# Two gated convolution layers and a linear attention: the normalization between layers, split into three chunks and one

## The chip, the cores and the metric

The kernel runs on one core of one Trainium2 chip, in float32. The metric is the device time of one execution in microseconds (us), as the median of several executions.

## The reference

The input has 512 channels of 64 x 64 pixels. Four layers follow each other, each as `x = x + layer(_gn(x))`, where `_gn` normalizes groups of 16 channels over all pixels:

```python
def _gn(v, G=32, eps=1e-5):
    g = v.reshape(B_, G, C_ // G, H_, W_)
    m = jnp.mean(g, axis=(2, 3, 4), keepdims=True)
    s = jnp.var(g, axis=(2, 3, 4), keepdims=True)
    return ((g - m) / jnp.sqrt(s + eps)).reshape(v.shape)

# layer 0: attention with 8 heads over 4096 pixels
# layers 1 and 2, gated convolutions:
fused = conv1x1(x, w_in, b_in)                  # 512 -> 1024 channels
pwa, abc = fused[:, :128], fused[:, 128:]
dw0, dw1, dw2 = dwconv7(abc, dw_w, dw_b)        # 7x7 per channel, 128 + 256 + 512 channels
h = pwa * dw0
h = conv1x1(h, pw0_w, pw0_b) * dw1
h = conv1x1(h, pw1_w, pw1_b) * dw2
return conv1x1(h, w_out, b_out)                 # 512 -> 512
# layer 3: linear attention; begins with qkv0 = conv1x1(x, w_qkv) * s_qkv + b_qkv (512 -> 768)
```

## The kernel before

The activations stay on the chip the whole time, as `X[128, 4, 4096]`: the 512 channels are four chunks of 128 partitions, the pixels are eight blocks of 512. A group of 16 channels lies inside one chunk, so the chunks can be normalized independently of each other.

**The normalization** is not written out as a pass of its own. The mean is taken off the pixels in place (`centered.take`, L355 on ACT, L357 on DVE and GpSimd), and the reciprocal deviation is multiplied into the weights of the layer that follows (L363 and L366 for `w_in`, L1316 for `w_qkv`). What both need comes from `_group_params`: the statistics of each chunk are aggregated on DVE (L95), a small product with a mask gives the negative mean of each group, `less` (L106, L108), another gives the variance (L115), then a square root on ACT (L121), a reciprocal and a correction step on DVE (L123 to L129) give `rstd`. The chain alternates between DVE, TensorE and ACT and is run once for each layer over all four chunks.

**The end of a gated layer.** The last of its output products take the hidden chunks `h5` and `h6` (`output` with chunks 5 and 6, after the gate products `g[5] + g[6]`). There is one output product for each of eight pixel blocks and four output chunks, 32 in all, blocks outside and chunks inside. After each, DVE adds the result to X (L1167) and takes the statistics of that block (L1169). A chunk's statistics are complete only with the last block.

**The beginning of the next layer.** `_group_params` runs; then the weights are scaled and the first four blocks of products are made, each over the four input chunks (`fused`, L842: `w_in[0]` and `w_in[1]`, or `w_qkv[0]` and `w_qkv[1]`, times pixel blocks 0 and 1). The other pixel blocks are centred meanwhile (`taken`). Products over the other blocks follow in a scheme with seven products instead of eight (`_Seven`), which needs sums of weights (L406) and differences of pixel blocks (L419) from DVE. The products become planes in DRAM, from which the depthwise convolution reads them back.

**The order of the work.** Each engine executes its own list in order. The lists come from a scheduler that reorders the program text by readiness; the big products of these layers are kept in the order of the text (`keep_in_program_order`), the small ones of the normalization are not. A product instruction of this kernel in float32 is executed as two TensorE instructions in the profile. DMAs are issued on three queues: SP (weights, taps, planes read back), ACT (planes written, `s_qkv`, `w_proj`) and GpSimd. Buffers come from pools that are stacked on each other; a new pool's buffers lie where closed pools' buffers were, and wait for those that used them last.

Of the whole kernel, the boundary between the two gated layers lies at about 2762 us of the profile, that between the second gated layer and the linear attention at about 3250 us.

Of the kernel before, what the change touches and what calls it, by code (L numbers as in the profile page):

```python
# [10 lines left out]
FP = mybir.dt.float32  # L11
AF = mybir.ActivationFunctionType
# [4 lines left out]
P = 128  # L17
# [75 lines left out]
def _aggregate(nc, mv, stats, c):  # L93

    nc.vector.bn_aggr(mv[:, c, :], stats[:, c, :, :].rearrange("p b s -> p (b s)"))  # L95


def _group_params(nc, small, psum, stats, gmask, known=None, mv=None):


    if mv is None:
        mv = small.tile([P, NC, 2], FP, tag="gn_mv", name="gn_mv")
        for c in range(NC):
            _aggregate(nc, mv, stats, c)
    ps = psum.tile([P, BLK], FP, tag="mm", name="gn_ps")
    nc.tensor.matmul(ps[:, 0:NC], gmask, mv[:, :, 0], start=True, stop=True)  # L106
    less = small.tile([P, NC], FP, tag="gn_less", name="gn_less")
    nc.vector.tensor_scalar(less, ps[:, 0:NC], -1.0, None, ALU.mult)  # L108

    d = small.tile([P, NC], FP, tag="gn_d", name="gn_d")  # L110
    nc.vector.tensor_add(d, mv[:, :, 0], less)
    nc.vector.tensor_mul(d, d, d)
    nc.vector.tensor_add(d, d, mv[:, :, 1])
    ps = psum.tile([P, BLK], FP, tag="mm", name="gn_ps")
    nc.tensor.matmul(ps[:, 0:NC], gmask, d, start=True, stop=True)  # L115
    if known is not None:
        known(less)
    a = small.tile([P, NC], FP, tag="gn_a", name="gn_a")
    nc.vector.tensor_scalar(a, ps[:, 0:NC], GN_EPS, None, ALU.add)
    s = small.tile([P, NC], FP, tag="gn_s", name="gn_s")  # L120
    nc.scalar.activation(s, a, AF.Sqrt)  # L121
    r = small.tile([P, NC], FP, tag="gn_r", name="gn_r")
    nc.vector.reciprocal(r, s)  # L123

    t = small.tile([P, NC], FP, tag="gn_t", name="gn_t")
    nc.vector.tensor_mul(t, r, r)
    nc.vector.tensor_mul(t, t, a)
    nc.vector.tensor_scalar(t, t, -0.5, 1.5, ALU.mult, ALU.add)
    nc.vector.tensor_mul(r, r, t)  # L129
    return less, r  # L130


@with_exitstack
def trunk_kernel(ctx: ExitStack, tc: tile.TileContext, a: dict, out: bass.AP):
# [56 lines left out]

    stats = _gated_convs(tc, a, X, vcol, vall, gmask, small, new_stats, centered, stats, mv, F)
    _linear_attention(tc, a, X, vcol, vall, ident, gmask, small, centered, stats, F3, Z, out)


# [132 lines left out]
class _Centered:  # L328
# [4 lines left out]
    def __init__(self, tc, small):  # L333
# [3 lines left out]
        self.nc.vector.memset(self.offset, 0.0)  # L337

    def first(self, view):


        def known(less):
            self.less = less
            for c in range(NC):
                self.take(view(c), c, (None, None, self.nc.gpsimd, self.nc.vector)[c])

        return known
# [10 lines left out]

    def scaled(self, w, rstd, eng):

        if eng is self.nc.scalar:
            for c in range(NC):
                eng.activation(w[:, c], w[:, c], AF.Copy, scale=rstd[:, c : c + 1])  # L363
        else:
            shape = [P, NC, w.shape[-1]]
            eng.tensor_tensor(w, w, rstd.unsqueeze(2).to_broadcast(shape), ALU.mult)  # L366
        return w


def _normalize(tc, X, gmask, small, psum, st):  # L370

    nc = tc.nc
    for b in range(NB):
        for c in range(NC):
            nc.vector.bn_stats(st[:, c, b, :], X[:, c, ts(b, BLK)])
    less, rstd = _group_params(nc, small, psum, st, gmask)
    for b in range(NB):
        for c in range(NC):
            xs = X[:, c, ts(b, BLK)]
            nc.vector.tensor_scalar(  # L380
                xs, xs, less[:, c : c + 1], rstd[:, c : c + 1], ALU.add, ALU.mult
            )
# [94 lines left out]
def _attention_pairs(tc, a, X, QO, gmask, small, centered, stats, mv, okay):  # L477
# [19 lines left out]
    with tc.tile_pool(name="att1", bufs=1) as p1, tc.tile_pool(  # L497
# [12 lines left out]
        for b in range(NB):  # L510
            for c in range(NC):
                nc.vector.bn_stats(stats[:, c, b, :], X[:, c, ts(b, BLK)])
        _, rstd = _group_params(
            nc, small, ps_mm, stats, gmask, centered.first(lambda c: X[:, c, 0:BLK])
        )


# [297 lines left out]
class _PlaneConv:  # L815
# [28 lines left out]
    def pixels(self, x, k):  # L844


        split = XW // self.f.phx
        v = x.rearrange("p (y h x n) -> p y h x n", y=XH, h=split, x=XW // split)
        py, px = divmod(k * self.pair, self.f.phx)
        return v[:, py, :, px : px + self.pair, :].rearrange("p h x n -> p h (x n)")  # L850

# [138 lines left out]


@with_exitstack
def _gated_convs(ctx, tc, a, X, vcol, vall, gmask, small, new_stats, centered, stats, mv, F):
# [11 lines left out]
    pc = _PlaneConv(ctx, tc, FORM, F, ps_cv, NL, 4, False)  # L1005

    for layer in ("L1", "L2"):
        pre = f"{layer}_conv_"

        def weights(name, i):  # L1010
# [9 lines left out]
        nc.sync.dma_start(out=pw1, in_=a[f"{layer}_pw1"])  # L1020
        _, rstd = _group_params(
            nc, small, ps_mm, stats, gmask, centered.first(lambda c: pc.pixels(X[:, c, :], 0)), mv
        )
        stats, mv = new_stats(), None

        centered.scaled(w_in[0], rstd, nc.vector)
        centered.began()
        for w in w_in[1:]:
            centered.scaled(w, rstd, nc.scalar)

# [7 lines left out]

        def taking(w, k):

            return product(lambda c: w[:, c, :], [pc.pixels(X[:, c, :], k) for c in range(NC)])

        def taken(k):
            for c in range(NC):
                centered.take(pc.pixels(X[:, c, :], k), c)

        def fused(i, k):

            put(i, k, taking(w_in[i], k), None)

# [165 lines left out]
        g = [blocks(gate, i) for i in range(NDW)]  # L1216
        fused(0, 0)
        taken(1)
        fused(1, 0)
        for b in (2, 3):  # L1220
            taken(b)
        fused(0, 1)
        for _ in made[0, 1]:
            pass
        fused(1, 1)
        for k in range(1, NB // 2):
# [8 lines left out]
        convolve(6, [], g[4] + outputs(4))  # L1235
        for _, f in g[5] + g[6] + outputs(5, 6):
            f()
    return stats


@with_exitstack
def _linear_attention(ctx, tc, a, X, vcol, vall, ident, gmask, small, centered, stats, F, Z, out):

# [10 lines left out]

    lq = ctx.enter_context(tc.tile_pool(name="lq", bufs=1))

    s_qkv = lq.tile([P, NQKV, P], FP, tag="s_qkv", name="s_qkv")
    nc.scalar.dma_start(
        out=s_qkv.rearrange("p i m -> p (i m)"),
        in_=bass.AP(a["L3_s"].tensor, a["L3_s"].offset, [[0, P], [1, NQKV * P]]),  # L1260
    )
    w_proj = lq.tile([P, NC, C], FP, tag="w_proj", name="w_proj")
    nc.scalar.dma_start(out=w_proj, in_=a["L3_w_proj"])
    ksum = small.tile([P, NC, NB], FP, tag="ksum", name="ksum")
# [33 lines left out]
    with ExitStack() as st:  # L1298
        wp = st.enter_context(tc.tile_pool(name="lw", bufs=1))
        w2p = st.enter_context(tc.tile_pool(name="lw2", bufs=4))  # L1300
        tmp = st.enter_context(tc.tile_pool(name="ltmp", bufs=5))
        kvp = st.enter_context(tc.tile_pool(name="kv", bufs=33))
        ps_vk = st.enter_context(tc.tile_pool(name="ps_vk", bufs=1, space=PSUM))
        ps_mm = st.enter_context(tc.tile_pool(name="ps_mm", bufs=4, space=PSUM))
        pc = _PlaneConv(st, tc, f, F, ps_mm, NL, 4, True)

        def weights(i):
# [5 lines left out]

        def scaled(i, w):
            for c in range(NC):
                nc.vector.scalar_tensor_tensor(  # L1316
                    w[:, c], w[:, c], rstd[:, c : c + 1], s_qkv[:, i], ALU.mult, ALU.mult
                )
            return w
# [15 lines left out]

        _, rstd = _group_params(
            nc, small, ps_mm, stats, gmask, centered.first(lambda c: pc.pixels(X[:, c, :], 0))
        )

        def product(w, hs):  # L1340
# [5 lines left out]
        for i, w in enumerate(w_qkv):  # L1346
            scaled(i, w)
        centered.began()

        def taken(k):  # L1350
            for c in range(NC):
                centered.take(pc.pixels(X[:, c, :], k), c)

        def put(i, k, ps, more=None):
# [5 lines left out]
            )  # L1360

        def fused(i, k):
            w = w_qkv[i]
            ps = product(lambda c: w[:, c, :], [pc.pixels(X[:, c, :], k) for c in range(NC)])
            put(i, k, ps)

# [71 lines left out]
        def more_weights():  # L1438
# [3 lines left out]
        dve, pool = nc.vector, nc.gpsimd  # L1442
        made = [
            lambda: fused(0, 0),
            lambda: [taken(1), summed(0), fused(1, 0)],
            lambda: [taken(2), taken(3), fused(0, 1)],
            lambda: [[p() for p in differences(1, dve)], fused(1, 1)],
        ]
        made += group(0, 1, centers(2) + differences(2, dve))
        made += group(0, 2, centers(3) + differences(3, dve))  # L1450
# [149 lines left out]

        fill(33)
        convs([(0, 0), (1, 0)], fills(5, 5, 5, 5))
# [225 lines left out]
```

## Time and profile before

| | us |
|---|---|
| median of 3 executions | 3862.63 |
| lowest and highest | 3862.24, 3863.66 |
| the profiled execution | 3863.14 |
| its span | 3861.4 |
| mean granted TensorE clock in it | 0.996 of full speed |

The profile is that of one execution. Its page gives the busy time of each engine and the costliest groups of instructions; further views are the waits (who waited for whom, in a stretch of time), the timeline (instructions in order of time, equal ones merged with their number behind an x), and a table of stretches with the busy time of each engine and the granted clock. PE is TensorE's matmuls, PEld its weight loads, DVE VectorE, ACT ScalarE, POOL GpSimd, SP the queue of SyncE. A line number is that of the code before. A wait for several events is put down to the one that came last.

### The profile page before, as it was taken

How to read it: one execution, taken by the hardware profiler on the slowest of the kernel's cores; microseconds unless marked ns; L12 is line 12 of the kernel's file. 1: busy time of each engine (PE TensorE's matmuls, PEld its weight loads, DVE VectorE, ACT ScalarE, POOL GpSimd, SP SyncE). 2: the span in 40 equal slices, each digit the busy share in tenths (PEclk: the TensorE clock that was granted, in tenths of full speed). 3: DMA queues.
4: the chain of work that ended last, by engine and by line, in shares of the span. 5: the costliest groups of instructions: out<-in, count | busy, mean ns of one | idle time of the engine just before them, and what ended most of it. 6: DMA issues, size and time to landing. Idle time of an engine off the chain costs nothing. (4 is left out here: it accounts for less than half of the span.)

```text
span 3861.4 us, 81785 instructions
## 1 busy us (share of the span) xinstructions
PE 3776.3 (98%) x35438; PEld 1674.7 (43%) x35438; DVE 2647.3 (69%) x3194; ACT 2063.5 (53%) x2987; POOL 112.2 (3%) x94
## 2 busy tenths in 40 slices
PE   6999999999999999999999999999999999999999
PEld 4533335333354333353333334554445544455544
DVE  5678774777766777747776757766677667575535
ACT  3677763777736777636665655663256632354210
POOL 0000000000000000000000000000000000122110
PEclk9999999999999999999999999999999999999999
DMA  2000000000000000000000015762056721463334
GB/s 99 9 1 1 1 1 9 1 1 1 1 1 9 1 1 1 1 9 1 1 1 1 1 49 167 201 199 75 17 161 191 202 73 42 151 181 96 94 96 141
DMA packets 194012, 221.56 MB, mean 57 GB/s; under 512 B 13400, under 2 KB 138584, under 8 KB 193520
## 3 DMA queue, kind: packets, MB, share of 16 engines
q1 hardware_dynamic: 166832, 157.12, 14.7%
q10 hardware_dynamic: 26784, 59.11, 4.2%
q8 instruction: 280, 4.59, 0.5%
q14 instruction: 84, 0.69, 0.1%
q0 software_dynamic: 32, 0.06, 0.0%
HBM read 156.46 MB, written 59.77 MB: 56 GB/s over the span
## 5 line engine op out<-in xcount | busy, mean ns | idle before, releaser
L664 ACT ACTIVATE pt<-ps_s,A 128x512 f32<-128x512 f32 x2048 | 1284.5, 686 | 536.6 <-PE ps_s L656 529.0
L741 DVE TENSOR_TENSOR acc<-acc,pt 128x1024 f32<-128x1024 f32 x960 | 1177.8, 1227 | 324.0 <-ACT pt L664 296.1
L676 PE MATMUL av<-pt,V 64*64 64x512 f32 x8192 | 1112.3, 590 | 0.9 <-ACT pt L664 0.9
L656 PE MATMUL ps_s<-O,K 64*64 64x512 f32 x8192 | 1111.4, 589 | 0.0
L676 PEld LDWEIGHTS av<-pt,V 64*64 64x64 f32 x8192 | 339.5, 133 | 557.6 <-issue 525.8
L656 PEld LDWEIGHTS ps_s<-O,K 64*64 64x64 f32 x8192 | 333.9, 133 | 554.5 <-issue 307.6
L920 ACT COPY S<-S 32x1295 f32<-32x1295 f32 (+1 forms) x272 | 341.4, 1256 | 218.2 <-DMA S<-F 107.4
L842 PEld LDWEIGHTS ps_cv<-S,T 64*32 64x32 f32 x13824 | 193.2, 105 | 109.6 <-issue 70.5
L842 PE MATMUL ps_cv<-S,T 64*32 64x128 f32 x13824 | 231.5, 272 | 4.4 <-DVE turned L974 1.5
L842 PE MATMUL ps<-diff,w_sum 128*128 128x512 f32 x492 | 231.1, 601 | 3.4 <-DVE w_sum L406 2.0
L842 PE MATMUL ps<-h,w_out_L 128*128 128x512 f32 x512 | 228.7, 599 | 1.5 <-DVE X L1163 1.4
L419 DVE TENSOR_TENSOR diff<-X 128x512 f32<-128x512 f32 x200 | 133.4, 683 | 83.3 <-PE ps L842 42.4
L355 ACT ACTIVATE X<-X,gn_less 128x512 f32<-128x512 f32 x120 | 76.9, 711 | 176.3 <-DVE gn_less L108 176.2
L842 PE MATMUL ps<-X,w_in_L 128*128 128x512 f32 x304 | 148.3, 620 | 11.1 <-ACT kept L1085 5.9
L842 PEld LDWEIGHTS ps<-h,w_out_L 128*128 128x128 f32 x512 | 94.3, 190 | 120.2 <-issue 98.7
L842 PE MATMUL ps<-h,pw_L 128*128 128x512 f32 x320 | 143.6, 599 | 1.2 <-DVE h L1151 1.0
L974 DVE STREAM_TRANSPOSE h<-ps_cv 128x512 f32<-128x512 f32 x112 | 109.3, 1050 | 50.1 <-PE ps_cv L842 49.6
L419 DVE TENSOR_TENSOR diff<-X,diff 128x512 f32<-128x512 f32 x200 | 133.7, 683 | 12.0 <-PE ps L842 10.5
L842 PEld LDWEIGHTS ps<-diff,w_sum 128*128 128x128 f32 x492 | 90.0, 190 | 111.2 <-issue 100.8
L567 PEld LDWEIGHTS ps_v<-wqkv,X 128*128 128x128 f32 x1024 | 120.6, 194 | 18.0 <-issue 12.5
L567 PE MATMUL ps_v<-wqkv,X 128*128 128x128 f32 x1024 | 121.9, 278 | 0.0
L452 DVE TENSOR_TENSOR kept<-kept,ps 128x512 f32<-128x512 f32 x57 | 38.9, 682 | 117.1 <-ACT sq L631 77.6
(182 smaller groups left out, 3136.5 us busy)
## 6 DMA issues: line engine op xcount, KB each, us to landing
T<-in_L_T_dram SPq DMA_DIRECT2D x112, 384.0 KB, 4.3
F<-plane ACTq DMA_DIRECT2D x112, 324.0 KB, 3.4
S<-F SPq DMA_DIRECT2D x224, 162.0 KB, 4.6
row<-G SPq DMA_DIRECT2D x80, 272.0 KB, 3.6
S<-G SPq DMA_DIRECT2D x96, 153.0 KB, 4.1
G<-plane ACTq DMA_DIRECT2D x48, 289.0 KB, 2.4
T<-in_L_T_dram SPq DMA_DIRECT2D x48, 256.0 KB, 3.9
out_dram<-y SPq DMA_DIRECT2D x32, 256.0 KB, 2.0
```

The source lines that it names most:

```text
L355: self.nc.scalar.activation(xs, xs, AF.Identity, bias=less)
L419: yield eng.tensor_tensor(t[j][c], a(c), b(c), ALU.subtract)
L452: nc.vector.tensor_add(kept[1], kept[1], ps[2])
L567: nc.tensor.matmul(ps[:, ts(i, P)], X[:, c, ts(b * QT + i, P)], w[:, 2, c, :], start=(c == 0), stop=(c == NC - 1),)
L656: nc.tensor.matmul(ps[ts(half, D), ts(h, BLK)], K[rows, t * P + half * D : t * P + (half + 1) * D], QO[pair][rows, cols], start=True, stop ...
L664: exp = nc.scalar.activation(pt[:, ts(h, BLK)], ps[:, ts(h, BLK)], AF.Exp, bias=A[:, t, h : h + 1])
L676: nc.tensor.matmul(av[half][rows, :], V[keys, t, rows], pt[keys, ts(h, BLK)], start=(t == 0), stop=(t == NT - 1),)
L741: add = nc.vector.tensor_add(acc, acc if u > 1 else first, pt)
L842: self.tc.keep_in_program_order(self.nc.tensor.matmul(*args, **kw))
L920: nc.scalar.copy(second, first)
L974: nc.vector.transpose(out, src)
```

## The change

The output products of the chunks `h5` and `h6` are made output chunk by output chunk: all eight pixel blocks of chunk 0, then of chunk 1, and so on. So three chunks' statistics are complete while the products of the fourth still run. The normalization's chain becomes a class with a generator that can be run for a range of chunks and in pieces; for chunks 0 to 2 its pieces stand between the last eight output products, and the pixels of these three chunks are all centred there. The next layer scales the weights' rows of chunks 0 to 2, begins with the products of its first four blocks over these three chunks, with the pieces of the chain for chunk 3 between them, and then adds the products over chunk 3. In the linear attention the pools are opened in another order, so that `w_qkv`, `s_qkv` and `w_proj` get buffers that come free earlier, and their loads move ahead. GpSimd centres no block any more at these two boundaries. The first gated layer, after the attention, runs the chain for four chunks as before.

```diff
-def _group_params(nc, small, psum, stats, gmask, known=None, mv=None):
...
+class _Norm:
...
+    def params(self, c0, c1, stats, bank, known=lambda: None):
+        nc, n, mv, gmask = self.nc, c1 - c0, self.mv, self.gmask
+        less, r = self.less[:, c0:c1], self.r[:, c0:c1]
+        d, a, s, t = (self.tile(f"{v}{c0}", n) for v in "dast")
+        if not self.given:
+            for c in range(c0, c1):
+                _aggregate(nc, mv, stats, c)
+        yield
+        ps = bank()
+        nc.tensor.matmul(ps[:, 0:n], gmask, mv[:, c0:c1, 0], start=True, stop=True)
+        nc.vector.tensor_scalar(less, ps[:, 0:n], -1.0, None, ALU.mult)
+        nc.vector.tensor_add(d, mv[:, c0:c1, 0], less)
+        nc.vector.tensor_mul(d, d, d)
+        nc.vector.tensor_add(d, d, mv[:, c0:c1, 1])
+        yield
+        ps = bank()
+        nc.tensor.matmul(ps[:, 0:n], gmask, d, start=True, stop=True)
+        known()
+        nc.vector.tensor_scalar(a, ps[:, 0:n], GN_EPS, None, ALU.add)
+        nc.scalar.activation(s, a, AF.Sqrt)
+        nc.vector.reciprocal(r, s)
...
+def _first_blocks(pc, X, ws, bank, put, pieces, scale, meanwhile):
+    first = [(i, k, bank()) for k in range(2) for i in range(2)]
+    def add(i, k, ps, c):
+        pc.matmul(
+            ps, ws[i][:, c, :], pc.pixels(X[:, c, :], k), start=(c == 0), stop=(c == NC - 1)
+        )
...
+    next(pieces)
+    for n, (i, k, ps, c) in enumerate((*p, c) for p in first for c in range(NC - 1)):
+        add(i, k, ps, c)
+        if n in (3, 6):
+            next(pieces, None)
+    scale()
+    for f in meanwhile:
+        f()
+    for i, k, ps in first:
+        add(i, k, ps, NC - 1)
+        put(i, k, ps, None)
...
 def _gated_convs(...)
...
+        else:
+            ready = NC - 1
+            for w in w_in:
+                centered.scaled(w, norm.r, nc.scalar, 0, ready)
...
+        def centered_first():
+            centered.take(pc.pixels(X[:, NC - 1, :], 0), NC - 1, nc.vector)
+            centered.take(pc.pixels(X[:, NC - 1, :], 1), NC - 1)
+        def scale_last():
+            for n, w in enumerate(w_in):
+                centered.scaled(w, norm.r, nc.scalar if n else nc.vector, ready)
+        _first_blocks(
+            pc, X, w_in, lambda: ps_mm.tile([P, BLK], FP, tag="mm", name="ps"), put,
+            norm.params(ready, NC, old_stats, bank_gn, centered_first) if ready else None,
+            scale_last, [] if ready else [lambda: taken(1)],
+        )
...
-        for _, f in g[5] + g[6] + outputs(5, 6):
+        for _, f in g[5] + g[6]:
             f()
-    return stats
+        last = [lambda b=b, o=o: output((5, 6), b, o) for o in range(NC) for b in range(NB)]
+        for f in last[: (NC - 1) * NB]:
+            f()
+        norm = _Norm(nc, small, gmask)
+        centered.by(norm)
+        pieces = norm.params(0, NC - 1, stats, bank_gn)
+        next(pieces)
+        form = FORM if layer == "L1" else FORM3
+        for b, f in enumerate(last[(NC - 1) * NB :]):
+            f()
+            if b in (1, 3):
+                next(pieces, None)
+        for k in range(NB):
+            for c in range(NC - 1):
+                centered.take(_pixels(form, X[:, c, :], k), c)
+    return stats, norm
 
 def _linear_attention(...)
...
-        wp = st.enter_context(tc.tile_pool(name="lw", bufs=1))
-        w2p = st.enter_context(tc.tile_pool(name="lw2", bufs=4))
-        tmp = st.enter_context(tc.tile_pool(name="ltmp", bufs=5))
         kvp = st.enter_context(tc.tile_pool(name="kv", bufs=33))
...
         pc = _PlaneConv(st, tc, f, F, ps_mm, NL, 4, True)
+        w2p = st.enter_context(tc.tile_pool(name="lw2", bufs=4))
+        wp = st.enter_context(tc.tile_pool(name="lw", bufs=1))
+        lq = st.enter_context(tc.tile_pool(name="lq", bufs=1))
...
         for i, w in enumerate(w_qkv):
-            scaled(i, w)
-        centered.began()
+            scaled(i, w, 0, NC - 1)
...
+        _first_blocks(
+            pc, X, w_qkv, lambda: ps_mm.tile([P, BLK], FP, tag="mm", name="ps"), put,
+            norm.params(
+                NC - 1, NC, stats,
+                lambda: ps_vk.tile([P, BLK], FP, tag="vk0", name="gn_ps"), centered_first,
+            ),
+            scale_last,
+            [lambda: taken(2), lambda: taken(3), lambda: summed(0)] + differences(1, dve),
+        )
```

## The prediction

> **What bounds the kernel now.** I read the page first, then the matmul engine's waits, stretch by stretch, then the timeline at the two places that the change touches, then the granted clock there. The page (engine: busy us, share of the span, instructions):
>
> ```profile
> span 3861.4 us, 81785 instructions
> PE 3776.3 (98%) x35438; PEld 1674.7 (43%) x35438; DVE 2647.3 (69%) x3194; ACT 2063.5 (53%) x2987; POOL 112.2 (3%) x94
> ```
>
> TensorE is busy 98% of the span, so only its idle time and time at a lower clock can be won by a reordering. Its waits between 2730 and 3255 us, and the one that follows at 3256.8 (us in total, times, longest):
>
> ```profile
> PE gn_ps L115 <- DVE gn_d L113: 3.0, 2, 1.5
> PE ps L842 <- ACT w_in_L L363: 2.3, 1, 2.3
> PE gn_ps L106 <- DVE beta L1327: 2.0, 1, 2.0
> PE gn_ps L106 <- DVE gn_mv L95: 1.9, 1, 1.9
> PE ps L842 <- DVE w_qkv L1316: 2.1, 1, 2.1
> ```
>
> These five are the two boundaries: B1 between the gated layers (at 2762) and B2 before the linear attention (at 3250). At each, TensorE waits three times: for the last statistics, for the deviations, for the first scaled weight. The timeline of B1 and B2 (start, us, then the instruction; in brackets the idle time before it):
>
> ```profile
> 2764.32 0.39 PE L106 MATMUL gn_ps<-gn_mv,gmask 128*128 128x4 f32 x2 [1.92 <-DVE gn_mv L95]
> 2766.19 0.38 PE L115 MATMUL gn_ps<-gn_d,gmask 128*128 128x4 f32 x2 [1.49 <-DVE gn_d L113]
> 2768.89 18.16 PE L842 MATMUL ps<-X,w_in_L 128*128 128x512 f32 x36 [2.32 <-ACT w_in_L L363]
> 2768.15 3.60 ACT L363 ACTIVATE w_in_L<-w_in_L,gn_r 128x128 f32<-128x128 f32 x12
> 3255.04 7.44 ACT L355 ACTIVATE X<-X,gn_less 128x512 f32<-128x512 f32 x12
> 3256.18 1.14 DVE L1316 SCALAR_TENSOR_TENSOR w_qkv<-w_qkv,gn_r,s_qkv 128x128 f32<-128x128 f32 x4
> 3256.82 18.25 PE L842 MATMUL ps<-X,w_qkv 128*128 128x512 f32 x36 [2.12 <-DVE w_qkv L1316]
> ```
>
> B1: the last output product ends at 2762.41, the first of the next layer starts at 2768.89: 6.48 us. B2: 3250.43 to 3256.82: 6.39 us. To see beside it: 36 instructions take 18.2 us; at the steady spacing of 0.43 us they take 15.6. The clock (stretch, length, busy us of PE, PEld, DVE, ACT, POOL, then the granted clock, DMA share, GB/s) tells why:
>
> ```profile
> 2766.00:2767.00 1.00, 0.38 (x2) 0.30 (x2) 0.30 (x3) 0.46 (x3) 0.93 (x1) 1.00 0.00 0
> 2767.00:2768.00 1.00, 0.00 (x0) 0.00 (x0) 0.81 (x5) 1.00 (x3) 0.00 (x0) 0.53 0.00 0
> 2773.00:2774.00 1.00, 1.00 (x2) 0.34 (x1) 0.00 (x0) 0.00 (x0) 0.00 (x0) 0.56 0.00 0
> 2774.00:2775.00 1.00, 1.00 (x4) 0.50 (x3) 0.00 (x0) 0.00 (x0) 0.00 (x0) 1.00 0.00 0
> ```
>
> It halves at 2767.06 and is whole again at about 2773.9, 5.05 us after the first product: 2.5 us lost. At B2 it halves at 3255.08 and returns at 3262.0: 5.16 us, 2.6 lost. So a boundary costs about 9 us, and B1 and B2 together 18, 0.47% of the span.
>
> **What is the same.** The boundary ahead of the first gated layer (2272) keeps its order: the statistics of all four chunks at once, the same products. Only the bank of its small products changes. Cost nothing. The last output products are the same 32 (64 instructions), only chunk outside and block inside; each needs its own weight load in either order, and their blocks of h5 and h6 are finished before: I take 0. DVE's add and statistics keep pace in either order, 1.42 of the 1.72 us that an output takes.
>
> **The four small products.** Each boundary now has four instead of two, and in B2 all lie between big ones. A row near to it is in the linear attention, one column wide (min/median/max ns, first and last start):
>
> ```profile
> L842 PE MATMUL ps_pb<-vec,w_proj x32: 250/250/271, 3431.5 to 3435.0; 128*128 128x1 f32 x32
> ```
>
> 32 in 3.5 us: 0.11 us of TensorE each, 0.22 for a product of two instructions. If the next big weight load can't be drawn ahead, two loads of 0.19 would show: 0.4. I take 0.22, range 0.1 to 0.4; four cost B2 0.9 (0.4 to 1.6).
>
> **B1 step by step**, in the order that the built program has on each engine. Zero is the end of chunk 2's last product, 13.74 us (16 products of 0.859) ahead of the old end, at 2748.67.
> 1. DVE adds at 0.06, takes statistics 0.78 to 1.47, aggregates to 1.87. The first small product stands behind two outputs of chunk 3, at 3.44. Its result reaches DVE 0.42 later (2764.32 to 2764.74 before); "less" stands behind an add there: ready at 4.26.
> 2. ACT now has a list: six centrings, the root (its input is there at 7.9), eighteen more centrings, and only then the weights. The row above gives 12 centrings in 7.44, so 0.62 each. 4.3 + 6 x 0.62 = 8.05; root 0.1; 18 x 0.62 = 11.2: ACT comes to the first weight at 19.3 and has it at 19.7.
> 3. TensorE's output products end at about 14.2 (13.74 and two small products). Its order is then: the two small products of chunk 3, then the 12 products over chunks 0 to 2. They are behind both. The statistics of chunk 3 come 1.9 later, the deviations another 1.9, at 18.0; but the weight comes at 19.7. So the first product starts at 19.8, which is 2768.45 in the old times, 0.44 ahead of before. The idle time is not removed here: three chunks' centring and scaling stand in it.
> 4. The fourth chunk: its root stands on ACT behind twelve scalings (0.30 each) and a centring, done at 23.9; r at 25; the scaled columns on DVE at 25.3, on ACT at 26.2. TensorE reaches the fourth chunk after 12 products, partly at half clock: 32.8. No wait.
> 5. Clock: the gap is 5.6 us. From fall to rise it is 6.9 us at both boundaries[...]. I take the same fall and rise; then half of the 0.44 is won, **0.2 us**. [...] 1.92, 1.49 and 2.32 with 0.4 us products between them did halve it. I go by the row and keep 2.7 as the far end.
>
> After the first blocks ACT has less to do, for 24 of 32 centrings are past; but TensorE waits for nothing in the old trace from 2769 to 2787, so this wins nothing.
>
> **B2 step by step.** The same zero, at 3236.69.
> 1. "less" at 4.26, root at 8.25, r of three chunks at 10.44 on DVE.
> 2. Here the weights are scaled on DVE, 12 at 0.27, and they are queued between the adds and statistics of blocks 5 to 7: scaling, add, scaling, statistics, and so on; the last six stand ahead of the final aggregate. Every add behind them comes later. Summing starts (0.27 a scaling, 0.60 an add, 0.61 statistics) from 10.48: adds of blocks 5, 6, 7 at 10.75, 12.5, 14.3; last statistics at 15.17, six scalings 15.78 to 17.37, aggregate to 17.74. Before it was 15.6.
> 3. TensorE goes straight on at 14.0: the first product's weight was ready at 10.8, its centred block at 4.9 to 8, and w_qkv and s_qkv are loaded since the end of the convolution (see the last rival). It does four products to 17.47 and meets the small product, which waits for the aggregate until 17.8: **0.3 us stall**. Behind it are three products (2.6 us); the deviations need 1.9: no wait. Then five products, 4.3 us; r of chunk 3 needs ACT's root behind 20 centrings (20.7), then 1 us of DVE, and a scaling: 22.9. TensorE comes there at 25.1. No wait.
> 4. Sum: before, the first pair after the 16 products starts at 3273.19 (36th at 3274.48, less three spacings). After: 3250.28 + 0.44 small products + 0.3 stall + 0.44 + 13.74 = 3265.2 to 3265.3. **7.9 us won**: 6.4 idle and 2.6 clock, less 1.2. [...] the trace has 5.16 us at half, so 2.6.
> 5. Next: the planes of blocks 0 and 1 are written 0.86 us apart instead of 3.4, and two blocks share a plane that a DMA must first read. ACT then waits about 2.5 us for a landing, with "kept" of the next group behind it, ready at about 17.4 after TensorE's old end; TensorE needs it at 18.1. Cover 0.7 us; if it is gone, the price is what is over, under 1 us. POOL loses two centrings (1.6 to 1.9 us each) that nobody waited for on TensorE. SP moves four w_qkv loads ahead of the taps' loads; the taps are used first after 3300.
>
> Everything after B2 goes by TensorE's progress, so it moves as a whole. Sum 8.1. The profiled execution took 3863.14 (span 3861.4 and 1.7 around it), 0.5 above the median 3862.63; 3863.14 less 8.1, less 0.5: **3854.5**. Unknowns: small products 0.7, DVE's chain 0.7, clock phase 1: 3853.0 to 3856.2 for this case.
>
> **Rivals.**
> - Both boundaries are covered, as the change says: B1 too wins 6.5 + 2.5 - 0.8 = 8, time 3846.5. For it: the same construction. Against: ACT's 24 x 0.62 = 14.9 us from 4.3 on ends 5 us after TensorE's last output, and the weights are behind. 0.07.
> - B1 stays at full clock[...]: 3852.0. 0.09.
> - B2's DVE is later than summed (a scaling at its full 0.34, adds late, so that the stall is 2 us, or a plane's landing holds "kept"): 3857 to 3859. 0.11.
> - The edit does nothing in time: new waits of the moved buffers eat B2. 3862.5. 0.03.
> - Slower: w_qkv's loads are late. The first scaling waits for its load at the head of DVE's queue; adds 5 to 7, the statistics and chunk 3's norm are all behind it. If the four loads go out only when they do now (3250.51) and land after the 8.0 us that the slowest took, the first scaling is at 3258.5, the aggregate 7.3 later at 3265.8, the rest at half clock to 3268.7: the next group at about 3277 against 3273.2, time 3866.5. It decides against the change from a landing at about 3255. Against it: the pool was moved to where conv buffers lay, whose last product ends at 3153.6, and SP has the loads behind the last conv loads. 0.02.
>
> The main case has 0.68.
>
> **Numbers.** A measurement here tells about 0.2% from no change, 7.7 us, so the line is at 3854.9, inside the main case: I give 0.46 of its 0.68 below it. Faster 0.46 + 0.07 + 0.09 = 0.62; slower 0.02; within 0.36. The range leaves out the first rival, nothing and slower, and parts of the third: 3851.5 to 3858.0.
>
> **What would show it.** Right: at B2 no idle gap over 1 us and the granted clock 1.00 throughout; at B1 a gap of 5 to 6 us with ACT's scaled weight as the last releaser, ACT with 18 centrings in a row just ahead, clock at half for some 5 us after it. Wrong: B1's products starting within 2 us of the last output; at B2 a wait of over 1 us of the small product for the aggregate, or of a "kept"; any wait of DVE for w_qkv's load.

## The result and the profile after

| | before, us | changed, us | ratio, 95% interval |
|---|---|---|---|
| side by side on one chip, 13 runs each | 3863.66 (3860.18 to 3868.36) | 3855.16 (3853.39 to 3857.97) | 0.9977 (0.9969 to 0.9986) |
| again on another occasion, 11 and 7 runs | 3865.39 (3860.79 to 3869.11) | 3854.60 (3854.19 to 3856.63) | 0.9972 (0.9961 to 0.9984) |

The change wins 8.5 us by the medians, and the interval of the ratio leaves 5.4 to 12.0. The profiled run of the changed kernel is the slowest of its 13, 3857.97 us, so profile against profile shows only 5.2; the boundaries themselves have to be compared. From its page:

```profile
span 3856.2 us, 81818 instructions
PE 3774.7 (98%) x35446; PEld 1675.2 (43%) x35446; DVE 2645.7 (69%) x3214; ACT 2067.8 (54%) x2994; POOL 108.6 (3%) x92
```

TensorE has eight instructions more, the four small products that the two boundaries gained. (Line numbers are now those of the changed code: L124 and L132 are the small products, L125 `less`, L383 and L385 the centring, L135 the root, L391 the scaling of `w_in`, L1415 that of `w_qkv`, L879 the big products.)

TensorE's waits in the changed kernel from 2745 to 2790 us, then from 3236 to 3268 us (in total, times, longest):

```profile
PE gn_ps L124 <- DVE gn_mv L95: 2.0, 1, 2.0
PE ps L879 <- ACT w_in_L L391: 1.4, 1, 1.4
PE gn_ps L132 <- DVE gn_d L129: 1.2, 1, 1.2
...
PE gn_ps L124 <- DVE gn_mv L95: 0.2, 1, 0.2
```

At B1 all three waits of before are still there, 4.6 us instead of 5.7. At B2 one of 0.2 us is left. The timeline of TensorE at both:

```profile
2757.08 7.11 PE L879 MATMUL ps<-h,w_out_L 128*128 128x512 f32 x16
2766.20 0.35 PE L124 MATMUL gn_ps<-gn_mv,gmask 128*128 128x1 f32 x2 [2.01 <-DVE gn_mv L95]
2767.75 0.35 PE L132 MATMUL gn_ps<-gn_d,gmask 128*128 128x1 f32 x2 [1.20 <-DVE gn_d L129]
2769.52 18.32 PE L879 MATMUL ps<-X,w_in_L 128*128 128x512 f32 x36 [1.42 <-ACT w_in_L L391]
...
3252.42 3.60 PE L879 MATMUL ps<-X,w_qkv 128*128 128x512 f32 x8
3256.22 0.35 PE L124 MATMUL gn_ps<-gn_mv,gmask 128*128 128x1 f32 x2 [0.21 <-DVE gn_mv L95]
3256.43 2.82 PE L879 MATMUL ps<-X,w_qkv 128*128 128x512 f32 x6
3259.09 0.28 PE L132 MATMUL gn_ps<-gn_d,gmask 128*128 128x1 f32 x2
3259.23 9.69 PE L879 MATMUL ps<-X,w_qkv 128*128 128x512 f32 x22
```

B1: the outputs end at 2764.19, the first product comes at 2769.52, 5.33 us later, and the 36 instructions (the first sixteen products and the two after them) take 18.3 us as before. B2: the first product follows the outputs at once, the small products lie between big ones, and the 36 instructions have no gap but the 0.21. What fills the time at B1 is on ScalarE:

```profile
2754.28 3.78 ACT L383 ACTIVATE X<-X,gn_less 128x512 f32<-128x512 f32 x6 [72.64 <-DVE gn_less L125]
2757.97 0.19 ACT L135 ACTIVATE gn_s<-gn_a 128x3 f32<-128x3 f32 x1
2758.06 11.11 ACT L383 ACTIVATE X<-X,gn_less 128x512 f32<-128x512 f32 x18
2769.08 3.60 ACT L391 ACTIVATE w_in_L<-w_in_L,gn_r 128x128 f32<-128x128 f32 x12
```

Eighteen centrings in a row, 11.1 us, and only then the weights. The granted clock (the third number from the right) around B1, and over the whole of B2:

```profile
2767.00:2768.00 1.00, 0.25 (x2) 0.28 (x2) 0.60 (x4) 1.00 (x3) 0.00 (x0) 0.98 0.00 0
2768.00:2769.00 1.00, 0.10 (x1) 0.02 (x1) 0.16 (x1) 1.00 (x2) 0.00 (x0) 0.50 0.00 0
2774.00:2775.00 1.00, 1.00 (x3) 0.48 (x2) 0.68 (x4) 1.00 (x3) 0.00 (x0) 0.60 0.00 0
2775.00:2776.00 1.00, 1.00 (x3) 0.38 (x2) 1.00 (x3) 1.00 (x3) 0.00 (x0) 1.00 0.00 0
...
3250.00:3268.00 18.00, 17.79 (x46) 7.91 (x45) 15.20 (x45) 13.83 (x24) 2.14 (x4) 1.00 0.23 76
```

At B1 it falls to 0.50 at about 2768.0 and is whole again at 2774.8, 6.8 us later; at B2 it is 1.00 from 3250 to 3268.

**One ruler for all runs.** Zero is the end of chunk 2's last output product: 3.44 us before the first small product where the chain is split, 13.74 us before the last output's end where it is not. The distance from there to the first product of a pixel difference with `w_sum` (the start of the next group) holds the idle time and the half clock of a boundary together:

| kernel | B1, us | B2, us |
|---|---|---|
| before | 38.22 | 38.22 |
| changed | 37.84 | 30.53 |
| changed, second profile | 38.15 | 30.53 |
| B2 only | 37.68 | 30.52 |
| weights first (4 centrings ahead) | 30.08 | 30.52 |
| twelve centrings ahead | 34.02 | 30.53 |
| before, order of the outputs alone | 37.46 | 37.30 |
| before, idle time filled | 35.76 | 35.40 |

Against the profile of before the change wins 0.38 us at B1 and 7.69 at B2.

### The profile page after: what moved, and what is told of

It is laid out like the page before. It is cut to its first block, busy times and chain, and to the rows that moved or that the text cites. A ratio compares the mean times of both kernels' runs of the same rounds, so it can differ in the third digit from the quotient of the medians.

```text
span 3856.2 us, 81818 instructions
## 1 busy us (share of the span) xinstructions
PE 3774.7 (98%) x35446; PEld 1675.2 (43%) x35446; DVE 2645.7 (69%) x3214; ACT 2067.8 (54%) x2994; POOL 108.6 (3%) x92
## 5 line engine op out<-in xcount | busy, mean ns | idle before, releaser
L879 PEld LDWEIGHTS ps_cv<-S,T 64*32 64x32 f32 x13824 | 194.0, 105 | 111.1 <-issue 78.7
L879 PE MATMUL ps_cv<-S,T 64*32 64x128 f32 x13824 | 232.6, 273 | 5.8 <-issue 2.1
L879 PE MATMUL ps<-diff,w_sum 128*128 128x512 f32 x492 | 231.7, 602 | 3.1 <-DVE w_sum L437 1.9
L879 PE MATMUL ps<-h,w_out_L 128*128 128x512 f32 x512 | 229.6, 599 | 1.5 <-DVE X L1233 1.4
L879 PE MATMUL ps<-X,w_in_L 128*128 128x512 f32 x304 | 147.1, 615 | 13.3 <-ACT kept L1155 6.3
L383 ACT ACTIVATE X<-X,gn_less 128x512 f32<-128x512 f32 x122 | 77.1, 708 | 152.1 <-DVE gn_less L125 152.1
L879 PEld LDWEIGHTS ps<-h,w_out_L 128*128 128x128 f32 x512 | 94.0, 190 | 118.3 <-issue 96.5
L879 PE MATMUL ps<-h,pw_L 128*128 128x512 f32 x320 | 143.8, 599 | 1.4 <-DVE h L1221 1.1
L450 DVE TENSOR_TENSOR diff<-X,diff 128x512 f32<-128x512 f32 x200 | 133.6, 683 | 11.6 <-PE ps L879 10.8
L879 PEld LDWEIGHTS ps<-diff,w_sum 128*128 128x128 f32 x492 | 90.3, 190 | 111.4 <-issue 101.5
```

Of the source, the lines that this page charges most:

```text
L383: self.nc.scalar.activation(xs, xs, AF.Identity, bias=less)
L450: yield eng.tensor_tensor(t[j][c], a(c), b(c), ALU.subtract)
L879: self.tc.keep_in_program_order(self.nc.tensor.matmul(*args, **kw))
```

## The experiments

**B2 alone.** The changed kernel with the first gated layer's end as before: outputs block by block, one chain over four chunks (and the statistics handed to it).

```
+        if layer == "L1":
+            for _, f in outputs(5, 6):
+                f()
+            norm = mv = None
+            continue
         last = [lambda b=b, o=o: output((5, 6), b, o) ...]
```

> The changed kernel with the boundary between the gated layers (B1) put back as it was: four chunks normalized at once, output products block by block; only the boundary before the linear attention (B2) is chunk by chunk. Theory: B2 carries nearly all of the gain and B1 only 0.2 to 0.4 us, so this is 7.4 to 8 us faster than the kernel before (about 3856) and within 0.5 us of the changed kernel. In its trace TensorE has no gap over 1 us at B2, and 6.5 us of idle and a halved clock at B1 as before. Rival: both boundaries give about half each, then this is about 4 us faster than before and 4 us slower than the changed kernel.

Measured: 3856.72 us against 3863.80, ratio 0.9983 (0.9976 to 0.9989), so 7.1 us by the medians. Its waits from 2745 to 2790 us are those of before:

```profile
PE ps L879 <- ACT w_in_L L391: 2.3, 1, 2.3
PE gn_ps L124 <- DVE gn_mv L95: 2.0, 1, 2.0
PE gn_ps L132 <- DVE gn_d L129: 1.6, 1, 1.6
```

and B2 is as in the changed kernel (30.52). The gain is B2's; half of 8.5 us for each boundary would give a time near 3859.5, a ratio of 0.9989, the very end of the interval, and the trace rules it out.

**The weights ahead of the centrings.** The changed kernel, but only two blocks of chunks 0 to 2 are centred at the first gated layer's end, so that four centrings and not eighteen stand between the root and the weights; the other blocks are centred in the next layer (`taken` runs over all chunks there).

```
         def taken(k):
-            for c in range(ready, NC):
+            for c in range(NC):
...
-        for k in range(NB):
+        for k in range(NB if layer == "L2" else 2):
             for c in range(NC - 1):
                 centered.take(_pixels(form, X[:, c, :], k), c)
```

> The changed kernel, but at B1 ScalarE centres only pixel blocks 0 and 1 of chunks 0 to 2 at the end of the layer; the other 18 centrings less 4 wait until the next layer's weights have been scaled. Theory: what keeps TensorE idle at B1 is ScalarE's list of 18 centrings (11.1 us) ahead of the weights. With four ahead instead, the first scaled weight is there some 8.7 us earlier (about 11 us after the end of chunk 2's last product), before TensorE has ended the outputs at 14.2: no gap over 1 us, clock 1.00 throughout, the next group of products starting 28.4 to 29 us after that zero instead of 36.1, and 7 to 7.7 us faster than the changed kernel, about 3847.5. Rival 1: the chain of the fourth chunk (statistics, deviations, root behind ScalarE's work) binds next, TensorE stops ahead of the fourth chunk's products by 2 to 5 us, gain 2 to 5. Rival 2: ScalarE's backlog is not what holds it, the gap stays at about 5 us, gain under 1.

Measured: 3847.20 us, ratio to before 0.9957 (0.9943 to 0.9971), 16.6 us under before and 8.0 under the changed kernel's median of the first table. ScalarE and TensorE at B1, in its timeline:

```profile
2758.49 0.19 ACT L135 ACTIVATE gn_s<-gn_a 128x3 f32<-128x3 f32 x1
2758.58 2.54 ACT L383 ACTIVATE X<-X,gn_less 128x512 f32<-128x512 f32 x4
2761.11 3.61 ACT L391 ACTIVATE w_in_L<-w_in_L,gn_r 128x128 f32<-128x128 f32 x12
2764.63 6.42 ACT L383 ACTIVATE X<-X,gn_less 128x512 f32<-128x512 f32 x10
...
2757.60 7.11 PE L879 MATMUL ps<-h,w_out_L 128*128 128x512 f32 x16
2764.55 3.60 PE L879 MATMUL ps<-X,w_in_L 128*128 128x512 f32 x8
2767.99 0.28 PE L124 MATMUL gn_ps<-gn_mv,gmask 128*128 128x1 f32 x2
2768.12 2.82 PE L879 MATMUL ps<-X,w_in_L 128*128 128x512 f32 x6
2770.78 0.28 PE L132 MATMUL gn_ps<-gn_d,gmask 128*128 128x1 f32 x2
2770.92 9.69 PE L879 MATMUL ps<-X,w_in_L 128*128 128x512 f32 x22
```

The weights begin 8.5 us earlier on this ruler (2761.11 less 2750.37, against 2769.08 less 2749.84), the first product follows the last output, the fourth chunk's small products wait for nothing, and the clock is 1.00 throughout. ScalarE does the same centrings later, beside products. The chain of the fourth chunk was not what held B1; the order of ScalarE's list was. This is the version that beats both kernels, and it comes close to the 3846.5 us that the prediction's first rival gave for two covered boundaries.

**Twelve ahead.** The same kernel with `2` changed to `6`: 12 centrings stand ahead of the weights.

> The kernel with the weights first at B1, but with 12 centrings ahead of the weights on ScalarE in place of 4 (the changed kernel has 18). Theory: each centring ahead of the weights delays them by 0.62 us, nothing else: the first scaled weight at 11.1 + 8 x 0.62 = 16.0 us after the end of chunk 2's last product, TensorE's outputs end at 14.2, so the gap is about 2 us, and the next group starts 2 us later than with four ahead, at about 30.4 after that zero. The clock: if one gap of about 2 us is too short to halve it, that is all, and the time is about 2 us above the kernel with four ahead (3849); if it halves, 2.5 more (3851.5). Rival: it is not the position of the weights in ScalarE's list; then the gap is 0 as with four or 5 as with eighteen.

Measured: 3848.11 us, ratio 0.9954 (0.9940 to 0.9968). ScalarE has the first weight at 15.9 us, as summed (16.0): the scaling begins 4.82 us later than with four ahead, 0.60 for each of the eight centrings. But the first product waits for something else, as TensorE's timeline shows:

```profile
2756.90 7.11 PE L879 MATMUL ps<-h,w_out_L 128*128 128x512 f32 x16
2766.02 0.35 PE L124 MATMUL gn_ps<-gn_mv,gmask 128*128 128x1 f32 x2 [2.00 <-DVE gn_mv L95]
2766.24 7.95 PE L879 MATMUL ps<-X,w_in_L 128*128 128x512 f32 x14
```

and afterwards the clock is low, in the table of stretches:

```profile
2766.00:2767.00 1.00, 0.98 (x4) 0.70 (x5) 0.55 (x3) 1.00 (x5) 0.00 (x0) 0.96 0.00 0
2767.00:2768.00 1.00, 1.00 (x2) 0.34 (x1) 0.42 (x4) 1.00 (x5) 0.00 (x0) 0.50 0.06 16
2770.00:2771.00 1.00, 1.00 (x3) 0.52 (x2) 0.00 (x0) 1.00 (x3) 0.00 (x0) 0.84 0.00 0
```

With weights this late the order on TensorE puts the first small product of chunk 3 ahead of the big ones, and that waits for its statistics until 16.35 us. There is this one gap of 2.0 us, and the clock falls at 2766.9 and returns at 2770.3: 3.4 us at half, which cost 1.7. Together the next group is 3.94 us later than with four ahead (34.02 against 30.08), where the sum was 2 or 4.5. Of these, 2.6 to 3.2 are left at the zero of B2, against the two profiles with four ahead. The medians (3848.11; 3847.20 and, on the same occasion, 3847.32 with four ahead) do not resolve it.

**The clock alone.** The kernel before, with 7, 5 and 8 products of the mask with itself in the three stretches in which TensorE waits at B1 and B2; their results are unused. `idle(n)` makes n of them, each two instructions of 128 columns; they and the small products of the chain are kept in the order of the text.

```
+    idle(7)
     ps = psum.tile([P, BLK], FP, tag="mm", name="gn_ps")
-    nc.tensor.matmul(ps[:, 0:NC], gmask, mv[:, :, 0], start=True, stop=True)
+    mm(ps[:, 0:NC], gmask, mv[:, :, 0])
+    idle(5)
...
-    nc.tensor.matmul(ps[:, 0:NC], gmask, d, start=True, stop=True)
+    mm(ps[:, 0:NC], gmask, d)
+    idle(8)
```

> The kernel before, with 7, 5 and 8 small products of the groups' matrix with itself (128 columns, results unused) put into the three stretches at B1 and at B2 in which TensorE waits. The order and the waits of everything else stay. Theory: half of what B2 won is idle time and a quarter to a third is the halved clock that follows it, so filling the idle time alone keeps the clock at 1.00 and gives back 2.5 us at each boundary, 5 us in all: about 3858.6, the first big product of each boundary starting when it does now (up to 0.4 us later where a filler is still running), and 36 instructions taking 15.6 us instead of 18.2. Rival: the halved clock does not come from the idle time or such small products do not count as work: clock still at half, time equal or 0.5 to 1 us longer.

Measured: 3860.20 us, ratio 0.9992 (0.9984 to 1.0000), 3.6 us by the medians and not told from 0 or from 5. B1 in its timeline:

```profile
2767.68 2.03 PE L106 MATMUL warm<-gmask 128*128 128x128 f32 x16
2770.13 15.69 PE L856 MATMUL ps<-X,w_in_L 128*128 128x512 f32 x36 [0.42 <-ACT w_in_L L377]
```

and the clock in the stretches around B1 and B2:

```profile
2762.00:2778.00 16.00, 14.95 (x67) 9.19 (x66) 7.93 (x24) 11.04 (x25) 1.85 (x1) 1.00 0.00 0
3250.00:3266.00 16.00, 15.30 (x67) 9.31 (x66) 13.59 (x48) 10.63 (x18) 3.71 (x5) 1.00 0.46 176
```

The first product comes as late as before (6.49 us after the outputs at B1, 6.48 before), and the 36 instructions take 15.7 us in place of 18.2. With the idle time filled the clock was 1.00 in both stretches, so the half clock of these boundaries came from the idle time, and filling that alone wins 2.5 us at B1 and 2.8 at B2 against the profile of before (0.25 of the latter because the first product itself came earlier), 1.7 and 1.9 against that of the next experiment.

**The order alone.** The kernel before with its last 32 output products chunk outside, block inside.

```
-        for _, f in g[5] + g[6] + outputs(5, 6):
+        for _, f in g[5] + g[6]:
             f()
+        for o in range(NC):
+            for b in range(NB):
+                output((5, 6), b, o)
```

> The kernel before with only the order of the last 32 output products changed, chunk outside and block inside, and the whole four-chunk chain after them. Theory: worth 0 (within 0.5 us), both boundaries keep their 6.4 us of idle and the halved clock. Rival: the order itself carries part of the gain (fewer stalls of weight loads, or statistics that end earlier), 1 us or more; or it costs, since chunk 3's statistics all come in the last four products: up to 1 us slower.

Measured: 3864.18 us, ratio 0.9998 (0.9990 to 1.0007). The order itself is worth nothing that can be seen. Its boundaries show something else: the same waits, but 17.2 us for the 36 instructions in place of 18.2.

```profile
2769.04 17.20 PE L842 MATMUL ps<-X,w_in_L 128*128 128x512 f32 x36 [2.31 <-ACT w_in_L L363]
3257.27 17.13 PE L842 MATMUL ps<-X,w_qkv 128*128 128x512 f32 x36 [2.12 <-DVE w_qkv L1319]
```

The half clock costs 1.5 us at each place where it cost 2.5 and 2.6 before. On the ruler, with the time at which the clock is whole again:

| profile, boundary | first product | clock whole again | next group |
|---|---|---|---|
| before, B1 | 20.22 | 25.21 | 38.22 |
| before, B2 | 20.13 | 25.29 | 38.22 |
| order alone, B1 | 20.43 | 23.47 | 37.46 |
| order alone, B2 | 20.33 | 23.24 | 37.30 |
| B2 only, B1 | 20.56 | 23.77 | 37.68 |
| changed, B1 | 19.68 | 24.96 | 37.84 |
| changed, second profile, B1 | 19.68 | 25.59 | 38.15 |

In every row the next group comes 15.5 us after the mean of the two times, to within 0.02 us. The first product depends mainly on the kernel: 19.68 us in both profiles of the changed one. The return does not follow it: there it came at 24.96 and at 25.59, and at B1 over all rows at 23.47 to 25.59. What sets it is not shown. By it alone, half of the difference, the same boundary costs up to 1.1 us more or less in these profiles.

**The boundary that was to cost nothing.** In both profiles of the changed kernel, and in those of the three kernels made from it so far, the first product of the first gated layer comes 9.73 to 9.75 us after the end of the attention (taken at the small product that follows its last big one, at 2272.01 in the profile of before and 2270.66 in the changed one), and 8.52 to 8.73 in the kernel before and the two made from it. TensorE and ScalarE there in the kernel before:

```profile
2280.53 18.29 PE L842 MATMUL ps<-X,w_in_L 128*128 128x512 f32 x36 [2.71 <-DMA pw_L<-in_L_pw_dram]
2276.93 1.28 ACT L121 ACT_TABLE_LOAD   x1
2278.22 0.20 ACT L121 ACTIVATE gn_s<-gn_a 128x4 f32<-128x4 f32 x1
```

and in the changed one:

```profile
2280.40 17.11 PE L879 MATMUL ps<-X,w_in_L 128*128 128x512 f32 x36 [3.99 <-DMA pw_L<-in_L_pw_dram]
2276.69 1.28 ACT L135 ACT_TABLE_LOAD   x1 [0.93 <-DVE gn_a L134]
2277.99 0.20 ACT L135 ACTIVATE gn_s<-gn_a 128x4 f32<-128x4 f32 x1
```

The trace has a table load of 1.28 us on ScalarE ahead of the root. Before, the load ran while the root's input was being made; now it waits for that input (the bracket on the load). The brackets on TensorE's lines name a DMA, but the second profile of the changed kernel has the same wait for `w_in`, L391. In the changed program the root has two things to wait for, its input and ScalarE's own earlier use of the buffer by the attention's root, and the wait for the input stands ahead of the load. The kernel before reuses its buffer too, but its root keeps the wait for the input alone, behind the load; why only the changed program keeps the second is not shown. The edit, on top of the weights-first kernel:

```
-        d, a, s, t = (self.tile(f"{v}{c0}", n) for v in "dast")
+        d, a, t = (self.tile(f"{v}{c0}", n) for v in "dat")
+        s = self.tile("s_given" if self.given else f"s{c0}", n)
```

> The kernel with the weights first at B1 and four ahead, and in addition the tile that the root writes ahead of the first gated layer has a buffer of its own. In the changed kernel and in all made from it ScalarE's table load for that root waits for the root's input (VectorE's gn_a) and the first product comes 9.74 us after the end of the attention, where the kernel before had the load done ahead of it and 8.5 to 8.7. Theory: the reused buffer gives the root a second thing to wait for, and the first wait is put on the table load; with a buffer of its own the load does not wait, the root is 1.0 to 1.2 us earlier and the first product comes at 8.5 to 8.8. As the first products there run at half clock, about half of it is won, 0.5 to 0.6 us: the next group starts 26.3 to 26.7 us after the end of the attention instead of 27.0 to 27.3. Time about 3846.7, too little to be seen in the medians. Rival: the load waits for something else, no change.

Measured: 3847.32 us, ratio 0.9951 (0.9937 to 0.9964); against 3847.20 nothing to be seen, as expected. Its timeline:

```profile
2277.03 1.28 ACT L136 ACT_TABLE_LOAD   x1
2278.32 0.20 ACT L136 ACTIVATE gn_s_given<-gn_a 128x4 f32<-128x4 f32 x1
...
2280.74 18.29 PE L880 MATMUL ps<-X,w_in_L 128*128 128x512 f32 x36 [2.88 <-ACT w_in_L L392]
```

The load no longer waits and the first product comes 8.64 us after the attention: the second wait, for the reused buffer, was what held the load. The price follows from the same distance as at B1. The clock is at half there too: in the profiles of before, changed, B2 only, weights first, the clock alone and the order alone it returns 12.6 to 13.8 us after the attention's end, and the first difference product comes 15.5 us after the mean of first product and return, to within 0.02. So 1.1 us of delay costs half, 0.55. Without this the readings mislead: 26.32 to 26.65 us in the kernel before and the two made from it, 26.69 to 27.27 in the five profiles with the late load, and 26.76 here, just outside what was expected. By the 15.5 us the clock returned 13.9 us after the attention here, an estimate from 8.64 and 26.76, and later than in those six.

**The changed kernel again.**

> The changed kernel once more, as it is, beside the two others on one chip. Theory: as in its first profile, B1 with 5.3 us of gap and a halved clock, B2 with none, 9.7 us from the attention's end to the first gated layer's first product. What differs from its first profile (two stops of 1.2 and 1.5 us without a releaser in the first gated layer's body) is of the single run and is not there again, or elsewhere. Time 8 us under the kernel before, within 2 us. Rival: those stops belong to the changed kernel and come back at the same place.

Measured: 3854.60 us (the second row of the first table); the weights-first kernel with the root's own buffer took 3847.32 on the same occasion, 7.3 less. B1 and B2:

```profile
2770.41 18.64 PE L879 MATMUL ps<-X,w_in_L 128*128 128x512 f32 x36 [1.42 <-ACT w_in_L L391]
...
3252.76 3.60 PE L879 MATMUL ps<-X,w_qkv 128*128 128x512 f32 x8
```

Of the two stops without a releaser in its first profile (`ps` 1.5 us, `ps_cv` 1.2), `ps` does not come back and `ps_cv` does, 2.1 in two. The kernel before with the filled idle time has them too (2.1 and 1.3), and the order-alone kernel has 0.5. They come and go with the run, in both kernels; what they are stays open.

## Why the prediction was right, point by point

The forecast was 3854.5 us for 3855.16 and 3854.60, with B2 covered and B1 not.

- **B1, ScalarE's list.** Right: `less` ready at 4.40 us (4.26 forecast), the root at 8.1 (8.05), the weights at 19.2 (19.3), the first product at 19.68 (19.8), a gap of 5.3 (5.6). The weights-first kernel shows the cause and what it costs: 7.8 to 8.1 us of boundary.
- **B1, its 0.2 us.** Right in its mechanism: the first product comes 0.54 us earlier than in the profile of before (0.44 forecast), and half of that, 0.27, is what it wins when the clock returns at the same time. The same return was assumed and does not hold: at B1 it moved by 2.1 us among the profiles, which is 1.1 us of time, so single profiles set against each other show anything from a loss of 0.7 to a gain of 0.4.
- **B1, the clock.** Right: the timeline of before told it. With gaps of 2.0, 1.2 and 1.4 us the clock was at half for 6.8 us, in the twelve-ahead kernel with a single one of 2.0 for 3.4. The forecast's far end of 2.7 us for B1 and its rival of 3852.0 were estimates of B1 without this.
- **B2, its steps.** Right: first product at 14.19 us (14.0 and the small products), the aggregate done at 17.84 (17.74), the stall 0.21 (0.3), no wait at the deviations, none at chunk 3, no `kept` that TensorE waited for. Three small products cost 0.22 us each (two take the first product from 13.74 to 14.19); the one that waits costs 0.57 with its wait (0.5 forecast).
- **B2, its 7.9 us.** 7.69 against the profile of before. The term "2.6 for the clock" is the weak one: 2.6 is what one profile of before had, with a late return, and the order-alone kernel lost only 1.46 there. Against that profile B2 wins 6.8 us. So the 7.9 lies at the upper end of what these two profiles give up.
- **"The boundary ahead of the first gated layer ... cost nothing."** Wrong: 1.1 us later, about 0.6 in the end. The step rested on the order of the instructions, which is the same, and not on what each waits for.
- **A count.** Each of the 32 outputs at a layer's end is two products, one over `h5` and one over `h6`: 128 instructions in the trace, not the 64 of the prediction. Its 13.74 us for the last eight outputs has all sixteen products, so the sum is not touched.
- **The slower rival.** `w_qkv` is loaded from 3155.4 us on and landed at most 8.2 us after issue; its first scaling is at 3249.0. The cover is some 85 us.

The sum by the runs: B2 6.8 to 7.7, B1 0.3 to 0.4 by its first product, less 0.55, so 6.5 to 7.6 us. The medians say 8.5 and 10.8, with intervals that begin at 5.4 and 6.2; whether anything beyond the boundaries is won is not shown. The forecast's agreement to a microsecond is therefore partly luck: a clock term at its upper end and a missing loss.

## What to carry to other kernels

Splitting a chain so that its first part runs early helps only if what the next stage needs first is also first in the list of the engine that makes it: here eighteen centrings that nobody needed yet stood ahead of twelve weights, and moving them behind doubled the gain. Before calling an untouched stage free, compare what each instruction waits for, not only the order, since a second wait, for a reused small buffer, put a table load of 1.28 us on the path. And compare boundaries by when the first product starts: at B1 that was 19.68 us in both profiles of the changed kernel, while the clock came back at 24.96 and at 25.59.

## What the runs showed of the hardware

- The granted clock was 1.00 or 0.50 in the profiles of before and of the changed kernel. It was at half for 3.4 us after the gap of 2.0 us in the twelve-ahead kernel, for 6.8 us with the 4.6 to 5.9 us of waits at B1 and B2 (both in before, B1 in changed and in B2 only), and for 10.2 us with the 7.4 us of waits behind the attention in the profile of before.
- The fall does not lie at a fixed time after the outputs' end: it came 4.6 and 4.7 us after it at B1 and B2 in the profile of before, and 3.2 at B1 with B2 only, with nearly the same waits (5.7 and 5.9 us).
- At B1 only the part of the half clock behind the first product cost time, half its length: 3.0 us of it cost 1.5 with the order alone, 5.9 cost 3.0 in the changed kernel's second profile.
- The clock also fell where TensorE shows no wait: after the 32 products one column wide near the end (3431.5 to 3435.2 in the profile of before, 3425.4 to 3429.1 in that of the changed kernel) it fell 0.9 and 1.0 us after their end, for 3.4 us. Why is not shown.
- With 40 instructions of 128 columns, whose results nobody uses, in the 6.5 us between the outputs and the first product at B1, the clock stayed at 1.00 from 2762 to 2778.
- The table load ahead of the root took 1.28 us on ScalarE. Where it waited for the root's input, the first product came 9.74 us after the attention (changed kernel), and where it did not, 8.52 (before) and 8.64 (root's buffer of its own).
